# Mixing before projecting in a graph attention layer, with scores as dot products on VectorE and a new deadline for the list scheduler

## The chip, the cores and the metric

The kernel runs on one core of a Trainium2 chip. Times are device microseconds (us) of that core; a smaller number is better. The kernel before took 2403.49 us, the median of 3 runs (2402.94 to 2405.41). The names of lines (L404) are line numbers of the kernel that the profile belongs to; up to L576 the lines that matter have the same number in both.

## The reference, cut to what matters

The input is 64 graphs of 256 nodes with 256 features, and a 0/1 adjacency per graph. Two layers are applied, each to a normalised and rectified input, each with a residual.

```python
h = relu(layernorm(x))
for i in range(3):                              # layer 0: gated graph network
    m = h @ weight[i]
    aggr = A^T m                                # per graph
    h = gru_cell(aggr, h, w_ih, w_hh, b_ih, b_hh)
x = x + h
h = relu(layernorm(x))                          # layer 1: graph attention
h1 = h @ W.T
e = leaky_relu((h1 @ a_left)[:, None] + (h1 @ a_right)[None, :], 0.2)
alpha = softmax(where(adj == 0, -1e9, e))
x = x + alpha @ h1
```

## The kernel before

Two graphs make a pair; there are 32 pairs, and up to three are in work at once. The pieces that the argument touches follow, in the order of the program. Each call of `pe`, `dve`, `act` or `pool` gives an operation to a list, with an estimate of its cost in ns; nothing is issued then.

```python
# layer 0: split of h for the propagation, on GpSimd           (L495, L497)
pool(530,  ... nc.gpsimd.tensor_copy(nodes(hi)[:, sl, :], nodes(h)[:, sl, :]))
pool(1190, ... nc.gpsimd.tensor_sub(nodes(lo)[:, sl, :], nodes(h)[:, sl, :], nodes(hi)[:, sl, :].bitcast(F32)))
# [...] propagation (L512), then the gated layer's products (L404), summed on
# ScalarE (L411) and VectorE (L414)
# layer 0: the update, for each half db of the features        (L542 to L552)
dve(660,  ... scalar_tensor_tensor(u(), u(), b_h[...], r, op0=ALU.add, op1=ALU.mult))      # L542
dve(V512, ... tensor_add(u(), u(), feats(b)[:, 1, :]))                                       # L545
act(630,  ... activation(u(), u(), AF.Tanh, bias=...))                                       # L547
dve(V512, ... tensor_sub(d(), d(), u()))                                                     # L549
dve(V512, ... tensor_mul(d(), d(), z))                                                       # L550
dve(V512, ... tensor_add(d(), d(), u()))                                                     # L552
# layer 0: the new h back to node layout, 4 transposes a graph (L566)
pe(4 * TR, back, r=[(hT, (g, G + g))], w=[(pt, ONE)])
# [...]
# layer 1: norm, relu, to_features (4 transposes), projection with two score columns
norm_relu(xt, h, g)
to_features(h, hT, g)
pe(4 * 218, proj, r=[(hT, (g, G + g))] + WT, w=[(pm, ONE)])      # h W^T | h (W^T a)
# [...] scores, masked softmax
pe(4 * MM, mix, r=[(pT, ONE), (h1, ks)], w=[(pv, ONE)])          # alpha (h W^T)
```

The order on every engine comes from a list scheduler that runs when the kernel is built. Each operation gets a priority: the deadline of its pair, less the estimated time from the operation to the end of its chain. Among the operations that can start first, the one with the smallest priority goes first. Once built, each engine's order is fixed.

```python
def run(self, deadline):
    for o in reversed(self.ops):
        d = deadline(o.pair)
        for s in o.succs:
            d = min(d, s.prio)
        o.prio = d - o.lat
    # [...] while operations are left: the lowest (start, prio, seq) is placed

order = plan.run(lambda p: 30000.0 * max(p, 0))
```

So the numbers in the deadline are no time that is waited for. They only decide how the work of neighbouring pairs is interleaved. The estimates are constants.

## Time and profile before

| before | value |
|---|---|
| time | 2403.49 us |
| span of the profiled run | 2402.3 us |
| TensorE busy (PE) | 2366.8 us, 99% |
| VectorE busy (DVE) | 1671.0 us, 70% |
| ScalarE busy (ACT) | 1412.9 us, 59% |
| GpSimd busy (POOL) | 536.2 us, 22% |
| TensorE's waits from 100 to 2250 us | 3.2 us in 3 waits |
| one pair in the steady middle | 72.80 us |

In the steady middle one pair leaves the kernel at equal distances. I take the timeline of output transfers, the time from the 2nd to the 29th of them, divided by the 27 intervals: (2221.97 - 256.40) / 27 = 72.80 us. It separates what costs something for each pair from what costs something once, at the start or the end. The same 27 intervals are used for every kernel below.

### The profile page before, as it was taken

The numbers are of one execution on the slowest core, as the hardware profiler recorded it, in microseconds if no ns is written. First come the engines' busy times: TensorE is split into PE (matmuls) and PEld (weight loads), VectorE is DVE, ScalarE is ACT, GpSimd is POOL, SyncE is SP. The second block draws the span as 40 slices with busy tenths as digits, with TensorE's granted clock in tenths as the row PEclk, the third lists the DMA queues.
The fourth block names the chain that finished last, engine by engine and source line by source line (L and its number), as shares of the span: only waits on it lengthen the run. The fifth ranks groups of instructions, "written<-read, shape, count | busy, mean of one in ns | idle before, by whom it ended". The sixth has DMA issues, their size and how long they took to land.

```text
span 2402.3 us, 32347 instructions
## 1 busy us (share of the span) xinstructions
PE 2366.8 (99%) x12385; PEld 2097.8 (87%) x12385; DVE 1671.0 (70%) x3225; ACT 1412.9 (59%) x2757; POOL 536.2 (22%) x582
## 2 busy tenths in 40 slices
PE   8999999999999999999999999999999999999996
PEld 6888888888888888888888888888888888888885
DVE  5577776767676767667677767676767676777774
ACT  5465565665565665566655556655666655666653
POOL 3022222122222122222122222222221222221200
PEclk9999999999999999999999999999999999999998
DMA  3000000000000000000000000000000000000000
GB/s 114 1 10 27 27 27 27 17 11 27 27 27 27 7 21 27 27 27 27 1 27 27 27 27 18 10 27 27 27 27 10 18 27 27 27 19 1 10 9 18
DMA packets 53562, 55.02 MB, mean 23 GB/s; under 512 B 1680, under 2 KB 53408, under 8 KB 53408
## 3 DMA queue, kind: packets, MB, share of 16 engines
q1 hardware_dynamic: 53376, 52.96, 6.6%
q8 instruction: 97, 1.59, 0.3%
q14 instruction: 57, 0.47, 0.1%
q10 hardware_dynamic: 32, 0.01, 0.0%
HBM read 36.18 MB, written 16.78 MB: 22 GB/s over the span
## 4 chain that ended last, share of the span: by engine, by line
PE 96%; DVE 2%; ACT 1%; issue 0%; DMA 0%; POOL 0%; ACTq 0%; DVEq 0%; POOLq 0%
PE bank L404 72%; PE bank L512 7%; PE bank L649 5%; PE bank L594 4%; PE bank L566 4%; PE bank L473 2%; PE bank L640 1%; PE bank L605 1%; PE bank L335 0%; DVE full L552 0%; DVE full L549 0%; DVE small L445 0%; DVE full L550 0%; DVE full L542 0%; ACT full L624 0%
## 5 line engine op out<-in xcount | busy, mean ns | idle before, releaser
L404 PE MATMUL bank<-full,fac 128*128 128x256 f32 x4032 | 1015.2, 379 | 0.0
L404 PE MATMUL bank<-full,fac_hh 128*128 128x256 f32 x4032 | 988.8, 379 | 4.5 <-DVE full L552 3.4
L404 PEld LDWEIGHTS bank<-full,fac 128*128 128x128 f32 x4032 | 752.0, 190 | 95.1 <-DVE full L376 0.4
L404 PEld LDWEIGHTS bank<-full,fac_hh 128*128 128x128 f32 x4032 | 746.5, 190 | 96.8 <-DVE full L552 3.9
L414 DVE TENSOR_TENSOR full<-full,bank 128x512 f32<-128x512 f32 x576 | 386.3, 685 | 419.2 <-PE bank L404 400.2
L411 ACT COPY full<-bank 128x512 f32<-128x512 f32 x576 | 332.9, 584 | 331.7 <-PE bank L404 331.7
L372 POOL TENSOR_TENSOR full<-full 128x512 f32<-128x512 f32 x96 | 124.4, 1296 | 1146.4 <-DVE full L552 1085.0
L528 ACT ACTIVATE full<-full,b_rz 128x512 f32<-128x512 f32 x192 | 135.2, 721 | 222.6 <-DVE full L414 222.6
L512 PE MATMUL bank<-round,round 128*128 128x256 f32 x1536 | 249.1, 305 | 1.7 <-DVE round L576 1.7
L453 POOL TENSOR_TENSOR small<-small,nhalf 128x2 f32<-128x2 f32 x128 | 99.0, 787 | 605.0 <-DVE small L451 603.2
L512 PEld LDWEIGHTS bank<-round,round 128*128 128x128 f32 x1536 | 209.7, 190 | 12.0 <-DVE round L576 1.9
L460 ACT ACTIVATE full<-x,small 128x256 f32<-128x256 f32 x256 | 142.4, 594 | 59.1 <-DVE small L455 59.1
L547 ACT ACTIVATE full<-full,vec 128x512 f32<-128x512 f32 x192 | 133.0, 722 | 64.6 <-DVE full L545 64.3
L549 DVE TENSOR_TENSOR full<-full,full 128x512 f32<-128x512 f32 x192 | 132.0, 688 | 12.3 <-ACT full L547 12.3
L542 DVE SCALAR_TENSOR_TENSOR full<-full,vec,full 128x512 f32<-128x512 f32 x192 | 135.5, 747 | 2.7
L550 DVE TENSOR_TENSOR full<-full,full 128x512 f32<-128x512 f32 x192 | 131.2, 696 | 4.4
L531 ACT ACTIVATE full<-bank,b_rz 128x256 f32<-128x256 f32 x192 | 80.6, 471 | 87.1 <-PE bank L404 86.7
L516 ACT COPY full<-bank 128x512 f32<-128x512 f32 x192 | 109.9, 573 | 32.8 <-PE bank L512 32.8
L552 DVE TENSOR_TENSOR full<-full,full 128x512 f32<-128x512 f32 x192 | 124.6, 689 | 0.1
L545 DVE TENSOR_TENSOR full<-full 128x512 f32<-128x512 f32 x192 | 123.6, 684 | 0.0
L372 DVE TENSOR_TENSOR full<-full 128x512 f32<-128x512 f32 x96 | 66.6, 694 | 81.6 <-ACT full L516 81.6
L566 PE MATMUL bank<-ident,full 128*128 128x128 f32 x768 | 113.5, 277 | 7.1 <-DVE full L552 7.0
(76 smaller groups left out, 2362.2 us busy)
## 6 DMA issues: line engine op xcount, KB each, us to landing
x<-in_x_dram SPq DMA_DIRECT2D x32, 512.0 KB, 3.9
adj<-in_adj_dram SPq DMA_DIRECT2D x32, 512.0 KB, 3.9
out_dram<-x SPq DMA_DIRECT2D x32, 512.0 KB, 2.9
full<-in_L_gnn_w_ih_dram SPq DMA_DIRECT2D x2, 384.0 KB, 5.2
full<-in_L_gnn_weight_dram SPq DMA_DIRECT2D x3, 256.0 KB, 7.0
full<-in_L_gnn_w_hh_dram SPq DMA_DIRECT2D x2, 384.0 KB, 6.8
full<-in_L_gnn_W_dram SPq DMA_DIRECT2D x1, 256.0 KB
rows<-in_L_gnn_a_dram ACTq DMA_DIRECT2D x1, 2.0 KB
```

What stands on the lines that cost most here:

```text
L372: eng.tensor_sub(T.t[:, : 2 * N].rearrange("p (c n) -> p c n", c=2), q[:, :, 1, :], b.t[:, : 2 * N].rearrange("p (c n) -> p c n", c=2))
L404: nc.tensor.matmul(bank.t[:, ts(s, N)], fac[t[0]][:, f, t[1], :], quarter(srcs(t), q), start=(first and n == 0), stop=True, skip_group_che ...
L411: act(A512, lambda: nc.scalar.copy(quarters(dest[e])[:, :, g, :], both(X)), r=[(X, ONE)], w=[(dest[e], (g, 2 + g))])
L414: dve(V512, lambda: nc.vector.tensor_add(quarters(dest[e])[:, :, g, :], quarters(dest[e])[:, :, g, :], both(bank)), r=[(bank, ONE)], w=[(d ...
L460: act(495, lambda k=k, nb=nb: nc.scalar.activation(nodes(dst)[:, k, :], nodes(src)[:, k, :], AF.Relu, bias=sm.t[:, 18 + nb : 19 + nb], sca ...
L512: nc.tensor.matmul(pa.t[:, ts(db, N)], nodes(part)[:, k, ts(db, P)], Ar()[:, k, :], start=(n == 0), stop=(n == len(terms) - 1))
L528: act(630, lambda s=s, RZ=RZ: nc.scalar.activation(feats(RZ[0])[:, s, :], feats(RZ[0])[:, s, :], AF.Sigmoid, bias=b_rz[:, 2 * s : 2 * s + 1]),
L542: dve(660, lambda u=u, db=db, en=en, RZ=RZ: nc.vector.scalar_tensor_tensor(u(), u(), b_h[:, en : en + 1], feats(RZ[db])[:, 0, :], op0=ALU. ...
L547: act(630, lambda u=u, en=en: nc.scalar.activation(u(), u(), AF.Tanh, bias=b_i[:, en : en + 1]), r=[("vec", ONE)], w=[(U[db], (0, 1))])
L549: dve(V512, lambda u=u, d=d: nc.vector.tensor_sub(d(), d(), u()), r=[(U[db], (0, 1))], w=[(hT, q)])
L550: dve(V512, lambda d=d, b=RZ[db]: nc.vector.tensor_mul(d(), d(), feats(b)[:, 1, :]), r=[(RZ[db], (2, 3))], w=[(hT, q)])
L566: nc.tensor.transpose(pt.t[:, (nb * DB + db) * P : (nb * DB + db + 1) * P], feats(hT)[:, db, ts(g * NB + nb, P)], ident)
```

## The change

The intent is to save TensorE work. Since alpha (h W^T) = (alpha h) W^T, the softmax can mix h itself, in node layout, and project afterwards. Then h needs no transposed copy in layer 1. The two scores h (W^T a) become dot products on VectorE, with W^T a spread over all partitions once (`va`). Besides, the deadline gets a slope of 32000 in place of 30000, and the last two pairs get nearly one deadline.

```diff
-            to_features(h, hT, g)
             ks = (g * NB, g * NB + 1)
+            sm = sms[g]
             for nb in range(NB):
 [...]
-                pe(4 * 218, proj, r=[(hT, (g, G + g))] + WT, w=[(pm, ONE)])
-                act(320, lambda pm=pm, k=k: nc.scalar.copy(h1v()[:, k, :], pm.t[:, : D + 2]), ...)
+                for n in range(2):
+                    c = 12 + n * NB + nb
+                    dve(395, lambda ...: nc.vector.scalar_tensor_tensor(
+                        nodes(sc)[:, k, :], nodes(h)[:, k, :], 1.0, va[:, n, :], op0=ALU.mult, op1=ALU.mult,
+                        accum_out=sm.t[:, c : c + 1]), ...)
 [...]
-            pe(4 * MM, mix, r=[(pT, ONE), (h1, ks)], w=[(pv, ONE)])
+            pe(4 * MM, mix, r=[(pT, ONE), (h, ks)], w=[(pg, ONE)])
+            act(A512, lambda ag=ag, pg=pg: nc.scalar.copy(ag.t[:, : DB * N], pg.t), r=[(pg, ONE)], w=[(ag, ONE)])
+            pe(4 * MM, project, r=[(ag, ONE)] + WT, w=[(pv, ONE)])
 [...]
-        order = plan.run(lambda p: 30000.0 * max(p, 0))
+        order = plan.run(lambda p: 32000.0 * (max(p, 0) - 0.7 * max(0, p - (NPAIR - 2))))
```

Cut are the setup of `va` in place of two columns of `wT`, the score operations that now read `sm`, and the renamed buffers.

More of the change, by code (lines that the diff above doesn't have):

```diff
@@ L188, in tile_gated_gnn_then_gat @@
     plan = Plan(WINDOW)
-    WIDE = NBLK * (D + 2)
+    WIDE = NBLK * D
     plan.slot_class("full", [const.tile([P, WIDE], F32, name=f"full{i}") for i in range(23)])
@@ L238, in tile_gated_gnn_then_gat @@
     fac = {m: const.tile([P, 7, 3, P], F32, name=f"fac_{m}") for m in ("hh", 0, 1, 2)}
-    wT = const.tile([P, DB, D + 2], F32, name="wT")
+    wT = const.tile([P, DB, D], F32, name="wT")
+    va = const.tile([P, 2, D], F32, name="va")
     X, ADJ = {}, {}
@@ L344, in setup, with go @@
         transposed(lambda c: wT[:, c, :D], lambda c, r0: ("wT", (c,)), W_n)
-        for db in range(DB):
-            pl = Buf("bank")
-            def go(db=db, pl=pl):
+        pl = Buf("bank")
+        def go():
+            for n in range(2):
                 for ob in range(DB):
-                    nc.tensor.matmul(pl.t[:, 0:2], nodes(Wb)[:, ob, ts(db, P)],
-                                     vec[:, : 2 * DB].rearrange("p (s o) -> p s o", o=DB)[:, :, ob],
+                    c = n * DB + ob
+                    nc.tensor.matmul(pl.t[:, ts(n, D)], vec[:, c : c + 1].to_broadcast([P, P]), nodes(Wb)[:, ob, :],
                                      start=(ob == 0), stop=(ob == DB - 1))
-            pe(440, go, r=[(Wb, ONE), ("vec", ONE)], w=[(pl, ONE)])
-            dve(70, lambda db=db, pl=pl: nc.vector.tensor_copy(wT[:, db, D : D + 2], pl.t[:, 0:2]),
-                r=[(pl, ONE)], w=[("wT", (DB + db,))])
-    WT = [("wT", (0, 1, 2, 3))]
+        pe(4 * MM, go, r=[(Wb, ONE), ("vec", ONE)], w=[(pl, ONE)])
+        dve(V512, lambda: nc.vector.tensor_copy(va, pl.t.rearrange("p (n d) -> p n d", n=2)), r=[(pl, ONE)], w=[("va", ONE)])
+    WT = [("wT", (0, 1))]
     B11, B12, B21, B22 = range(4)
@@ L577, in pair @@
                         nodes(lo)[:, sl, :], pv(), nodes(hi)[:, sl, :].bitcast(F32)), r=[(pt, ONE), (hi, ks)], w=[(lo, ks)])
-        h, hT, h1, sc, pm_ = (Buf("full") for _ in range(5))
-        h1v = lambda: h1.t.rearrange("p (k d) -> p k d", k=NBLK)
+        h, sc, pm_ = (Buf("full") for _ in range(3))
         sms = [Buf("small") for _ in range(G)]
@@ L585, in pair @@
             norm_relu(xt, h, g)
-            to_features(h, hT, g)
             ks = (g * NB, g * NB + 1)
+            sm = sms[g]
             for nb in range(NB):
-                k = g * NB + nb
-                pm = Buf("bank")
-                def proj(pm=pm, g=g, nb=nb):
-                    for db in range(DB):
-                        nc.tensor.matmul(pm.t[:, : D + 2], quarters(hT)[:, db, g, ts(nb, P)], wT[:, db, :],
-                                         start=(db == 0), stop=(db == DB - 1))
-                pe(4 * 218, proj, r=[(hT, (g, G + g))] + WT, w=[(pm, ONE)])
-                act(320, lambda pm=pm, k=k: nc.scalar.copy(h1v()[:, k, :], pm.t[:, : D + 2]), r=[(pm, ONE)], w=[(h1, (k,))])
+                for n in range(2):
+                    c = 12 + n * NB + nb
+                    dve(395, lambda k=g * NB + nb, n=n, c=c, sm=sm: nc.vector.scalar_tensor_tensor(
+                        nodes(sc)[:, k, :], nodes(h)[:, k, :], 1.0, va[:, n, :], op0=ALU.mult, op1=ALU.mult,
+                        accum_out=sm.t[:, c : c + 1]),
+                        r=[(h, (g * NB + nb,)), ("va", ONE)], w=[(sm, (c,)), (sc, (g * NB + nb,))])
@@ L601, in pair, with right @@
             pR = Buf("bank")
-            def right(g=g, pR=pR):
+            def right(sm=sm, pR=pR):
                 for nb in range(NB):
-                    nc.tensor.transpose(pR.t[:, ts(nb, P)],
-                                        h1v()[:, g * NB + nb, D + 1 : D + 2].to_broadcast([P, P]), ident)
-            pe(2 * TR, right, r=[(h1, ks)], w=[(pR, ONE)])
-            for k in ks:
-                act(410, lambda k=k, pR=pR: nc.scalar.activation(
-                    nodes(sc)[:, k, :], pR.t[:, :N], AF.Prelu, bias=h1v()[:, k, D : D + 1], alpha=LEAKY_SLOPE),
-                    r=[(pR, ONE), (h1, (k,))], w=[(sc, (k,))])
+                    c = 12 + NB + nb
+                    nc.tensor.transpose(pR.t[:, ts(nb, P)], sm.t[:, c : c + 1].to_broadcast([P, P]), ident)
@@ L613, in pair @@
+            pe(2 * TR, right, r=[(sm, (14, 15))], w=[(pR, ONE)])
+            for nb, k in enumerate(ks):
+                act(410, lambda k=k, nb=nb, pR=pR, sm=sm: nc.scalar.activation(
+                    nodes(sc)[:, k, :], pR.t[:, :N], AF.Prelu, bias=sm.t[:, 12 + nb : 13 + nb], alpha=LEAKY_SLOPE),
+                    r=[(pR, ONE), (sm, (12 + nb,))], w=[(sc, (k,))])
             sl = slice(g * NB, (g + 1) * NB)
-            sm = sms[g]
-            dve(690, lambda sl=sl: nc.vector.copy_predicated(
+            dve(730, lambda sl=sl: nc.vector.copy_predicated(
@@ L616, in pair @@
                 nodes(pm_)[:, sl, :], nodes(A).bitcast(I32)[:, sl, :], nodes(sc)[:, sl, :]),
                 r=[(A, ks), (sc, ks)], w=[(pm_, ks)])
-            dve(620, lambda sl=sl, sm=sm: nc.vector.tensor_reduce(
+            dve(610, lambda sl=sl, sm=sm: nc.vector.tensor_reduce(
                 sm.t[:, 0:NB], nodes(pm_)[:, sl, :], AX.X, ALU.max, negate=True), r=[(pm_, ks)], w=[(sm, ONE)])
@@ L634, in pair @@
                 r=[(sm, (1,))], w=[(sm, (2,))])
-            pt, pT, pv = Buf("bank"), Buf("full"), Buf("bank")
+            pt, pT, pg, ag, pv = Buf("bank"), Buf("full"), Buf("bank"), Buf("full"), Buf("bank")
             def turn(g=g, pt=pt):
@@ L644, in pair, with mix, project @@
             dve(V512, lambda pt=pt, pT=pT: nc.vector.tensor_copy(pT.t[:, :GN], pt.t), r=[(pt, ONE)], w=[(pT, ONE)])
-            def mix(g=g, pT=pT, pv=pv):
+            def mix(g=g, pT=pT, pg=pg):
+                for db in range(DB):
+                    for jb in range(NB):
+                        nc.tensor.matmul(pg.t[:, ts(db, N)], nodes(h)[:, g * NB + jb, ts(db, P)], pT.t[:, ts(jb, N)],
+                                         start=(jb == 0), stop=(jb == NB - 1))
+            pe(4 * MM, mix, r=[(pT, ONE), (h, ks)], w=[(pg, ONE)])
+            act(A512, lambda ag=ag, pg=pg: nc.scalar.copy(ag.t[:, : DB * N], pg.t), r=[(pg, ONE)], w=[(ag, ONE)])
+            def project(ag=ag, pv=pv):
                 for ib in range(NB):
-                    for jb in range(NB):
-                        nc.tensor.matmul(pv.t[:, ts(ib, D)], pT.t[:, (jb * NB + ib) * P : (jb * NB + ib + 1) * P],
-                                         h1v()[:, g * NB + jb, :D], start=(jb == 0), stop=(jb == NB - 1))
-            pe(4 * MM, mix, r=[(pT, ONE), (h1, ks)], w=[(pv, ONE)])
+                    for db in range(DB):
+                        nc.tensor.matmul(pv.t[:, ts(ib, D)], ag.t[:, db * N + ib * P : db * N + (ib + 1) * P],
+                                         wT[:, db, :], start=(db == 0), stop=(db == DB - 1))
+            pe(4 * MM, project, r=[(ag, ONE)] + WT, w=[(pv, ONE)])
             for nb in range(NB):
```

## The prediction

> **What bounds the kernel now.** I read the page first: engine shares, and the chain that ended last.
>
> ```profile
> PE 2366.8 (99%) x12385; PEld 2097.8 (87%) x12385; DVE 1671.0 (70%) x3225; ACT 1412.9 (59%) x2757; POOL 536.2 (22%) x582
> ...
> PE 96%; DVE 2%; ACT 1%; issue 0%; DMA 0%; POOL 0%; ACTq 0%; DVEq 0%; POOLq 0%
> ```
>
> TensorE covers 99% of the 2402.3 us span and 96% of the chain, so only two things can move the time: the TensorE work itself, and the 2402.3 - 2366.8 = 35.5 us in which TensorE has nothing to do. Which line of the kernel is costly on VectorE or ScalarE matters only if TensorE ends up waiting for it. Next I asked where TensorE's idle time lies. The table of windows (start:end, length, then busy time per engine, granted clock, DMA share, GB/s) has it at the two ends:
>
> ```profile
> 0.00:20.00 20.00, 12.35 (x50) 8.28 (x51) 3.68 (x17) 9.63 (x22) 10.27 (x17) 0.91 0.77 249
> ...
> 2200.00:2250.00 50.00, 50.00 (x265) 44.55 (x264) 35.13 (x68) 29.38 (x57) 10.86 (x12) 1.00 0.03 11
> ...
> 2320.00:2340.00 20.00, 18.50 (x93) 15.60 (x92) 16.73 (x35) 12.25 (x26) 1.34 (x2) 1.00 0.00 1
> 2340.00:2360.00 20.00, 19.75 (x107) 17.13 (x106) 8.98 (x18) 10.25 (x21) 2.75 (x3) 1.00 0.08 27
> 2360.00:2380.00 20.00, 8.45 (x36) 6.42 (x34) 13.06 (x28) 6.85 (x13) 1.34 (x2) 0.69 0.00 0
> 2380.00:2402.30 22.30, 13.82 (x49) 10.17 (x47) 6.10 (x12) 7.60 (x20) 0.00 (x0) 0.81 0.07 24
> ```
>
> The start loses 7.65 us in its first 20 us. The middle is saturated: TensorE's waits between 100 and 2250 us add up to 3.2 us in three waits. From 2320 us on 1.50 + 0.25 + 11.55 + 8.48 = 21.8 us are lost. The timeline of the tail says why: the last gated-layer matmul (L404) of the last pair ends near 2364.1 us, and from there one dependent chain runs alone to 2402.3, that is 38.2 us, alternating between engines:
>
> ```profile
> 2371.75 2.36 PE L566 MATMUL bank<-ident,full 128*128 128x128 f32 x8 [6.84 <-DVE full L552]
> ...
> 2378.68 2.38 PE L473 MATMUL bank<-ident,full 128*128 128x128 f32 x8 [4.57 <-ACT full L460]
> ...
> 2390.22 0.33 PE L640 MATMUL bank<-ident,full 128*128 128x128 f32 x1 [3.06 <-ACT full L624]
> ```
>
> **A trap in the group table.** Its busy column cannot price a TensorE instruction, because the records overlap: the groups of one engine sum to more than its busy time. In a saturated stretch the distance between starts is the price:
>
> ```profile
> 1206.18 1.03 PE L404 MATMUL bank<-full,fac 128*128 128x256 f32 x4
> 1207.04 0.60 PE L566 MATMUL bank<-ident,full 128*128 128x128 f32 x4
> 1207.48 1.46 PE L404 MATMUL bank<-full,fac 128*128 128x256 f32 x6
> ```
>
> Four transposes move the next start by 0.44 us (110 ns each); four L404 records by 0.86 us (215 ns each). Averaged in the same way over the timeline from 300 to 2050 us: 109 ns for a transpose (L473 and L640: 108 to 109), 215.6 ns for an f32 record of 256 columns (L649 and L404), 217.9 ns for one of 258 columns (L594). An f32 matmul is two records (256 L649 matmuls in the program, 512 in the trace), so 431 ns; a transpose is one.
>
> [...] The trace has 427 (L376) and 689 (L552)[...]. The new dot products do ask for the accumulator; no run shows them yet.
>
> **The change part by part, TensorE.** Removed: the second to_features, 8 transposes per pair, 256 in all: 256 x 0.109 = 27.9 us. The projection of h (8 f32 matmuls per pair, 258 columns) becomes the projection of the mixed h (8 matmuls, 256 columns): 512 records x 2.3 ns = 1.2 us saved. The mix keeps 8 matmuls per pair. The row broadcast of the right scores keeps its 4 transposes per pair. Setup gets four matmuls of 256 columns in place of four of 2, some 0.8 us more. Net 27.9 + 1.2 - 0.8 = 28.3 us less TensorE work, all in the saturated stretch but for 0.9 us in the last pair's own tail.
>
> **VectorE and ScalarE.** VectorE gets 8 dot products per pair, 256 in all, over 128x256. By L542 and L376 I take 0.44 us each, and some 0.1 us for reading the accumulator, as ScalarE shows for its own (L624: 187 ns recorded, half hidden). 256 x 0.54 = 138 us, and 1671 becomes about 1810 us, 76% of the span. ScalarE loses 64 copies of the transposes (64 x 0.58 = 37 us) and 128 of the projection (45 us by its row), and gains 64 copies between mix and projection (37 us): about 1368 us. Neither becomes the bound; the work lies beside TensorE's except in the tail. "full" buffers become fewer per pair (hT and h1 go, two copies of the mix come), so buffer waits shouldn't grow.
>
> **The tail.** The built order of the changed kernel shows what the deadline does: both last pairs end their gated layers close together, and behind the last L404 lie the last pair's tail and most of the attention of the pair before: 12 transposes, 8 matmuls of its mix and 8 of its projection, which are 32 records. That is 12 x 0.109 + 32 x 0.2156 = 8.2 us of TensorE work that before stood ahead of that point and now falls into the chain's gaps. The 1.75 us lost at 2320 to 2360 us, which were waits for the same pair's attention, should mostly go too; I count 1.5.
>
> The chain itself, from the last L404, against 38.2 us before: VectorE now has the other pair's two copy_predicated (0.73 each) and two reduces (0.69) between L545 and L549, two dot products ahead of that, and a PSUM copy (0.68) behind: about +4.5 us until relu. From relu to the scores, transposes, copies and projections (2378.7 to 2386.8) become dot products that start behind each relu: 8 x 0.44 = 3.5 us, about 3.5 us less. The exps need no table load of their own (31 loads in the program for 32 before): -1.3. After the mix come a copy and the projection: 0.6 + 0.2 for the copy, 1.9 for the half that isn't overlapped: +2.7. Sum +2.4: a tail of about 40.5 us.
>
> **Sum.** The last L404 ends at 2364.1 - 27.4 (the saving outside the last tail) - 8.2 - 1.5 = 2327.0 us. I add 2 us for new waits in the middle, since VectorE's queue is fuller and its order was made for 0.395 us per dot product. With the tail: 2327.0 + 2 + 40.5 = 2369.5 us of span. The device time lies 1.2 us over the span (2403.49 against 2402.3): 2370.7, so 2371 us, 1.4% faster.
>
> **Rivals.** First, *VectorE becomes felt*. [...] For it:[...] the fixed order of the queue, which cannot move a late instruction aside. Against it: in the saturated middle VectorE waits 400 us in all for L404's banks, so it has room. [...] Second, *the tail gains more*: if the two pairs' chains overlap without queueing, the tail stays at 36 us or less and the time is 2364 to 2366. For it: the last 38 us hold 20 us of idle TensorE. Against it: the chain is one pair's dependences, and the other pair's work is queued in front of it on VectorE. Third, *a transpose is worth less than 109 ns*[...]. The distances between starts speak against it.
>
> **Range and chances.** The removed work is well priced (28 us, give or take 2); tail and new waits carry the doubt, some 10 us to each side, more upward. Range 2358 to 2386. Over 2% faster means below 2355.4, another 15 us of idle: 0.06. Over 2% slower would need VectorE to become the bound: 0.01. Within 2%: 0.93.
>
> **What would show it.** In the changed profile: TensorE busy near 2338 us with 256 L473 records; dot products of 0.4 to 0.5 us; TensorE waits in the middle below 6 us; the last L404 near 2329 us and 38 to 43 us behind it. I'm wrong if waits in the middle pass 15 us, if the dot products take 0.7 us, or if the tail leaves 36 to 46 us.

The sum came to 2327.0 + 2 + 40.5 = 2369.5 us of span, 2371 us of device time. The first rival's slower dot product and the third's cheaper transpose gave 2384 us each; neither was shown. (The 0.7 us among the tests at the end is the first rival's.) 427 and 689 are ns for 256 and 512 elements; L542 takes 747 ns for 512 in the trace. The trace of the kernel before shows:

- TensorE's groups add up to 2757 us of busy time, where the engine has 2366.8.
- Half of the accumulator's read by ScalarE (L624) is hidden: its 187 ns begin 94 ns before the activation ahead of it ends.
- A table load takes 1.283 us.
- The two-column matmuls of the setup (L350) start 111 ns apart. Eight records at 215.6 in place of eight at 111 make 0.84 us, the 0.8 of the sum.

The 2 us for new waits and the 0.2 us beside the copy are my estimates, with no line of the trace for them. That VectorE's queue keeps its order when an instruction is late is shown by two runs told below: the 20 instructions from an L414 to an L571 come in the same sequence in alg_only (from 996.22 us) and in late_casts (from 976.62), though two L549 take 0.69 and 0.68 us in the one, 1.76 and 1.75 in the other.

## The result, and the profile after

The changed kernel took 2448.16 us, the median of 6 runs (2446.94 to 2449.18), against 2403.44 for the kernel before in its 6 runs. The ratio is 1.0184, with a 95% interval of 1.0171 to 1.0197. A ratio here is the mean time of one kernel's fast runs over that of the other's of the same rounds, so it is not quite the ratio of the medians. The result is correct. The kernel is 1.8% slower, where 1.4% faster was predicted: 77 us over the prediction and 62 us beyond the range.

First the engine shares and the chain that ended last, of the kernel after:

```profile
PE 2369.6 (97%) x12129; PEld 2061.8 (84%) x12129; DVE 1790.4 (73%) x3736; ACT 1342.6 (55%) x2627; POOL 548.0 (22%) x582
...
PE 76%; DVE 18%; ACT 4%; issue 1%; DMA 0%; POOL 0%; ACTq 0%; DVEq 0%; POOLq 0%
```

TensorE runs the 256 matmul records fewer that it should (12129 for 12385). But 18% of the chain is now on VectorE, where it was 2%. The end of the program does not explain this. The last gated-layer matmuls are in TensorE's timeline:

```profile
2404.03 2.32 PE L404 MATMUL bank<-full,fac 128*128 128x256 f32 x10
```

The last of these ends near 2406.3 us of a span of 2446.6: a tail of 40.3 us, where 40.5 was predicted. The whole miss lies ahead of it: 2406.3 - 2329 = 77 us. Between 100 and 2260 us TensorE has these waits (the line it waits at, what it waits for, us in total, times, longest):

```profile
PE bank L566 <- DVE full L552: 43.9, 55, 1.3
PE bank L473 <- ACT full L460: 5.8, 1, 5.8
```

The first comes twice in each pair, about 1.3 us and then 0.3 us, all along: TensorE waits for the last step of the update before it can turn h back. By the output transfers a pair takes (2267.24 - 253.46) / 27 = 74.58 us, where 72.80 less the predicted saving of 0.90 would be 71.90. So 2.68 us are lost with each pair. The groups of VectorE instructions say which are longer (busy us, mean ns of one, then idle time before them); first before, then after:

```profile
L549 DVE TENSOR_TENSOR full<-full,full 128x512 f32<-128x512 f32 x192 | 132.0, 688 | 12.3 <-ACT full L547 12.3
L550 DVE TENSOR_TENSOR full<-full,full 128x512 f32<-128x512 f32 x192 | 131.2, 696 | 4.4
L545 DVE TENSOR_TENSOR full<-full 128x512 f32<-128x512 f32 x192 | 123.6, 684 | 0.0
```

```profile
L545 DVE TENSOR_TENSOR full<-full 128x512 f32<-128x512 f32 x192 | 166.6, 894 | 2.2
...
L550 DVE TENSOR_TENSOR full<-full,full 128x512 f32<-128x512 f32 x192 | 152.8, 823 | 2.2
...
L549 DVE TENSOR_TENSOR full<-full,full 128x512 f32<-128x512 f32 x192 | 139.6, 742 | 2.2 <-ACT full L547 2.2
```

These three lines are not touched by the change, and each does the same work as before. Yet the means rose by 210, 127 and 54 ns. There are 6 of each per pair, so 6 x 0.391 = 2.35 us per pair. The means mix two kinds: only one of the three updates of a pair is hit. Counted from the records of the trace, 56 of the 192 L545 have an L495 or L497 of GpSimd beside them for over 0.1 us and take 1400 ns in the mean; the others take 686. The new instructions, which I had watched, are as cheap as expected:

```profile
L591 DVE SCALAR_TENSOR_TENSOR full<-full,va 128x256 f32<-128x256 f32 x256 | 93.7, 420 | 19.8 <-ACT full L460 18.7
```

Here is one update in VectorE's timeline (start, duration, instructions in a row), before:

```profile
1004.60 1.42 DVE L542 SCALAR_TENSOR_TENSOR full<-full,vec,full 128x512 f32<-128x512 f32 x2
1005.93 1.29 DVE L545 TENSOR_TENSOR full<-full 128x512 f32<-128x512 f32 x2
1007.40 0.69 DVE L549 TENSOR_TENSOR full<-full,full 128x512 f32<-128x512 f32 x1 [0.19 <-ACT full L547]
1008.13 0.69 DVE L550 TENSOR_TENSOR full<-full,full 128x512 f32<-128x512 f32 x1
...
1010.07 1.29 DVE L552 TENSOR_TENSOR full<-full,full 128x512 f32<-128x512 f32 x2
```

and after:

```profile
1005.85 1.62 DVE L542 SCALAR_TENSOR_TENSOR full<-full,vec,full 128x512 f32<-128x512 f32 x2
1007.38 2.78 DVE L545 TENSOR_TENSOR full<-full 128x512 f32<-128x512 f32 x2
1010.08 1.09 DVE L549 TENSOR_TENSOR full<-full,full 128x512 f32<-128x512 f32 x1
1011.21 1.64 DVE L550 TENSOR_TENSOR full<-full,full 128x512 f32<-128x512 f32 x1
1012.77 0.68 DVE L549 TENSOR_TENSOR full<-full,full 128x512 f32<-128x512 f32 x1
1013.49 0.69 DVE L550 TENSOR_TENSOR full<-full,full 128x512 f32<-128x512 f32 x1
1014.10 1.29 DVE L552 TENSOR_TENSOR full<-full,full 128x512 f32<-128x512 f32 x2
```

From the start of L542 to the end of L552 it is 11.36 - 4.60 = 6.76 us before and 15.39 - 5.85 = 9.54 after. What else ran from 1007 to 1012 us? GpSimd's timeline of the kernel after:

```profile
1007.24 0.69 POOL L495 CAST round<-full 128x512 fp32r<-128x512 f32 x1 [4.25 <-ACT full L460]
1008.01 1.60 POOL L497 TENSOR_TENSOR round<-full,round 128x512 fp32r<-128x512 f32 x1
1009.56 1.07 POOL L495 CAST round<-full 128x512 fp32r<-128x512 f32 x1
1010.71 1.59 POOL L497 TENSOR_TENSOR round<-full,round 128x512 fp32r<-128x512 f32 x1
```

The four stand beside the long instructions of VectorE. As soon as the last one has ended, at 1012.3 us, L549 and L550 are back at 0.68 and 0.69. In the kernel before, the first pair of this group ran 10 us ahead of the update:

```profile
994.51 0.61 POOL L495 CAST round<-full 128x512 fp32r<-128x512 f32 x1 [2.42 <-ACT full L460]
995.20 1.27 POOL L497 TENSOR_TENSOR round<-full,round 128x512 fp32r<-128x512 f32 x1
```

There VectorE was idle, or in L414, which has one source in PSUM. An L414 that started at 995.49, within this L497, took 0.69 us, its usual time.

Nor was this one an exception: in the kernel before, 58 of the 576 L414 have an L495 or L497 beside them for over 0.1 us and take 688 ns in the mean, the others 684. In the kernel after, L549 and L550 with one beside them (27 of each) take 1092 and 1646 ns, the others 684 and 688. By the program L545, L549 and L550 have two inputs in SBUF, L414 has one, and L495 and L497 read SBUF. That two-input instructions of VectorE and instructions of GpSimd that read SBUF hold each other up was the theory, not shown so far, and the experiments had to show whether it carries the time.

### The profile page after: what moved, and what is told of

It reads as the page before. It is cut to its first block, busy times and chain, and to the rows that moved or that the text cites. A ratio compares the mean times of both kernels' runs of the same rounds, so it can differ in the third digit from the quotient of the medians.

```text
span 2446.6 us, 32271 instructions
## 1 busy us (share of the span) xinstructions
PE 2369.6 (97%) x12129; PEld 2061.8 (84%) x12129; DVE 1790.4 (73%) x3736; ACT 1342.6 (55%) x2627; POOL 548.0 (22%) x582
## 4 chain that ended last, share of the span: by engine, by line
PE 76%; DVE 18%; ACT 4%; issue 1%; DMA 0%; POOL 0%; ACTq 0%; DVEq 0%; POOLq 0%
PE bank L404 53%; PE bank L512 7%; PE bank L644 5%; PE bank L653 5%; PE bank L566 3%; DVE full L545 3%; DVE full L550 3%; DVE full L549 2%; DVE full L414 2%; DVE small L445 2%; DVE full L542 1%; ACT full L528 1%; PE bank L473 1%; PE bank L635 1%; DVE full L552 1%
## 5 line engine op out<-in xcount | busy, mean ns | idle before, releaser
L404 PE MATMUL bank<-full,fac_hh 128*128 128x256 f32 x4032 | 1024.2, 381 | 1.5 <-ACT full L411 1.5
L404 PE MATMUL bank<-full,fac 128*128 128x256 f32 x4032 | 1022.8, 380 | 0.1
L404 PEld LDWEIGHTS bank<-full,fac_hh 128*128 128x128 f32 x4032 | 746.8, 190 | 114.2 <-ACT full L411 22.1
L404 PEld LDWEIGHTS bank<-full,fac 128*128 128x128 f32 x4032 | 748.2, 190 | 103.0 <-DVE full L376 8.9
L414 DVE TENSOR_TENSOR full<-full,bank 128x512 f32<-128x512 f32 x576 | 378.5, 683 | 331.1 <-PE bank L404 308.1
L411 ACT COPY full<-bank 128x512 f32<-128x512 f32 x576 | 329.2, 583 | 356.6 <-PE bank L404 353.6
L372 POOL TENSOR_TENSOR full<-full 128x512 f32<-128x512 f32 x96 | 123.3, 1285 | 775.6 <-DVE full L552 594.2
L512 PE MATMUL bank<-round,round 128*128 128x256 f32 x1536 | 247.1, 303 | 1.8 <-DVE round L576 1.7
L512 PEld LDWEIGHTS bank<-round,round 128*128 128x128 f32 x1536 | 207.6, 190 | 18.1 <-DVE round L576 9.4
L528 ACT ACTIVATE full<-full,b_rz 128x512 f32<-128x512 f32 x192 | 129.0, 720 | 133.6 <-DVE full L414 133.4
L576 DVE TENSOR_TENSOR round<-bank,round 128x512 fp32r<-128x512 f32 x128 | 85.8, 689 | 118.1 <-ACT round L574 118.0
L545 DVE TENSOR_TENSOR full<-full 128x512 f32<-128x512 f32 x192 | 166.6, 894 | 2.2
L534 ACT ACTIVATE full<-full,b_rz 128x256 f32<-128x256 f32 x192 | 91.1, 506 | 138.2 <-DVE full L414 137.8
L566 PE MATMUL bank<-ident,full 128*128 128x128 f32 x768 | 114.2, 278 | 45.3 <-DVE full L552 45.2
L550 DVE TENSOR_TENSOR full<-full,full 128x512 f32<-128x512 f32 x192 | 152.8, 823 | 2.2
L566 PEld LDWEIGHTS bank<-ident,full 128*128 128x128 f32 x768 | 91.1, 141 | 72.9 <-DVE full L552 62.7
L542 DVE SCALAR_TENSOR_TENSOR full<-full,vec,full 128x512 f32<-128x512 f32 x192 | 140.8, 748 | 10.0
L460 ACT ACTIVATE full<-x,small 128x256 f32<-128x256 f32 x256 | 136.0, 592 | 14.8 <-DVE small L455 14.6
L549 DVE TENSOR_TENSOR full<-full,full 128x512 f32<-128x512 f32 x192 | 139.6, 742 | 2.2 <-ACT full L547 2.2
```

What stands on the lines that cost most here:

```text
L404: nc.tensor.matmul(bank.t[:, ts(s, N)], fac[t[0]][:, f, t[1], :], quarter(srcs(t), q), start=(first and n == 0), stop=True, skip_group_che ...
L411: act(A512, lambda: nc.scalar.copy(quarters(dest[e])[:, :, g, :], both(X)), r=[(X, ONE)], w=[(dest[e], (g, 2 + g))])
L414: dve(V512, lambda: nc.vector.tensor_add(quarters(dest[e])[:, :, g, :], quarters(dest[e])[:, :, g, :], both(bank)), r=[(bank, ONE)], w=[(d ...
L460: act(495, lambda k=k, nb=nb: nc.scalar.activation(nodes(dst)[:, k, :], nodes(src)[:, k, :], AF.Relu, bias=sm.t[:, 18 + nb : 19 + nb], sca ...
L512: nc.tensor.matmul(pa.t[:, ts(db, N)], nodes(part)[:, k, ts(db, P)], Ar()[:, k, :], start=(n == 0), stop=(n == len(terms) - 1))
L528: act(630, lambda s=s, RZ=RZ: nc.scalar.activation(feats(RZ[0])[:, s, :], feats(RZ[0])[:, s, :], AF.Sigmoid, bias=b_rz[:, 2 * s : 2 * s + 1]),
```

## The experiments

**The theory (C, collision).** The slope of 32000 moved GpSimd's casts and subtractions beside the update, both read SBUF, and the update is where TensorE then waits. **Rival V:** VectorE's queue is longer by the dot products, and the update comes late because of them. **Rival A:** the new algebra itself (the copy between mix and projection, fewer transposes for other work to hide behind) costs more than it saves. **Rival D:** the deadline is worse by itself, through the order on all engines, whatever GpSimd does. **Rival G:** it is not the reading, but simply that GpSimd is busy at that time.

All times in this table are medians, the ratio is to the kernel before on the same chip. The medians of before in the three groups of runs were 2404.28, 2404.61 and 2403.54 us. "Wrong" means a wrong result on purpose.

| kernel | us | ratio | us per pair | result |
|---|---|---|---|---|
| before | 2403.44 | 1 | 72.80 | correct |
| after | 2448.16 | 1.0184 | 74.58 | correct |
| alg_only | 2391.21 | 0.9945 | 71.90 | correct |
| deadline_only | 2415.8 | 1.0049 | 73.58 | correct |
| pool_blank | 2391.05 | 0.9943 | 72.53 | wrong |
| short_dots | 2446.76 | 1.0177 | 74.58 | wrong |
| slope30_tail | 2378.76 | 0.9890 | 71.90 | correct |
| slope32_flat | 2459.95 | 1.0229 | 74.60 | correct |
| pool_busy | 2390.55 | 0.9938 | 72.54 | wrong |
| late_casts | 2502.99 | 1.0408 | 75.11 | correct |
| after_late | 2422.9 | 1.0078 | 72.54 | correct |
| slope28_tail | 2391.01 | 0.9948 | 72.40 | correct |
| slope34_tail | 2424.97 | 1.0088 | 73.64 | correct |

### alg_only: the new algebra with the old deadline

```diff
-order = plan.run(lambda p: 32000.0 * (max(p, 0) - 0.7 * max(0, p - (NPAIR - 2))))
+order = plan.run(lambda p: 30000.0 * max(p, 0))
```

> The changed algebra with the old deadline (30000 per pair, no bend for the last two pairs). In the changed kernel a pair takes 74.58 us in the middle against 72.80 before and the 71.9 I had predicted, and TensorE waits for L552 once in each pair. If the new deadline made the order in which this happens, the middle falls to about 71.9 us per pair and the time to about 2376 us (27 us under before). If the algebra does it in any order, the time stays at 2445 to 2455 us.

It took 2391.21 us, ratio 0.9945 (0.9928 to 0.9961). A pair takes 71.90 us, 0.90 less than before. That is what the prediction's TensorE sum makes per pair, (27.9 + 1.2) / 32 = 0.91. The time missed the expected 2376 all the same: the middle gains 27 x 0.90 = 24 us, but the second output leaves 8.3 us later than in the kernel before (264.69 against 256.40), and from the 29th output to the end it is 3.8 us longer (184.1 against 180.3). L545, L549 and L550 are at 684, 689 and 693 ns. There is a collision in this order too: the dot products (L591) have a mean of 574 ns, and in the pair near 1015 us two of eight took 1.31 and 0.93 us beside GpSimd's L372 and L378, the others 0.41 or 0.42. TensorE waits for none of them from 300 to 2000 us. Rival A falls for the middle: the algebra gains there what it should, and the order is what takes it away.

### deadline_only: the kernel before with the new deadline

```diff
-order = plan.run(lambda p: 30000.0 * max(p, 0))
+order = plan.run(lambda p: 32000.0 * (max(p, 0) - 0.7 * max(0, p - (NPAIR - 2))))
```

> The kernel before with nothing but the new deadline. If the new slope of the deadline is to blame, this kernel gets the wait too, up to 2.7 us per pair, 2450 to 2480 us. If the algebra is to blame, it stays near 2400 us, a few us under or over before, by the tail alone.

It took 2415.8 us, ratio 1.0049 (1.0034 to 1.0064), 73.58 us per pair: 0.78 more than before. That is neither of the two times expected. L545, L549 and L550 stay at 691, 684 and 686 ns, so there is no collision here. Weight loads wait for other things (19.5 us for L376 in 47 waits, from 300 to 2000 us). Algebra alone is -0.90 per pair and the deadline alone +0.78; together they would be -0.12, but they measure +1.78. So 1.90 us per pair belong to neither part by itself, only to both together. Rival D holds for a smaller part.

### pool_blank: the same order, but GpSimd no longer reads

```diff
-pool(530, ... nc.gpsimd.tensor_copy(nodes(hi)[:, sl, :], nodes(h)[:, sl, :]), ...
+pool(530, ... nc.gpsimd.memset(nodes(hi)[:, sl, :].bitcast(F32), 0.0), ...
-pool(1190, ... nc.gpsimd.tensor_sub(nodes(lo)[:, sl, :], nodes(h)[:, sl, :], nodes(hi)[:, sl, :].bitcast(F32)), ...
+pool(1190, ... nc.gpsimd.memset(nodes(lo)[:, sl, :].bitcast(F32), 0.0), ...
```

The estimates given to the scheduler are kept, so the order on all engines is that of the kernel after. The moment is not: the cast waits for ScalarE's relu (L460, 4.25 us in the lines above), a memset of zeros doesn't, and so the memsets run earlier. The result is wrong (relative error 0.32).

> The changed kernel in exactly its own order on every engine, wrong on purpose: GpSimd's cast (L495) and subtraction (L497) of the first layer write zeros by memset, so that they read nothing from SBUF and are shorter. Theory 1, GpSimd and VectorE hinder each other: L545 falls from a mean of 894 ns to under 720, L550 from 823 to under 720, TensorE's wait for L552 nearly goes, the pair takes 72 to 72.5 us, the time is 2370 to 2385 us. Theory 2, VectorE is late because it has eight dot products more per pair: 2435 us or more.

It took 2391.05 us, ratio 0.9943 (0.9928 to 0.9958), and 72.53 us per pair: 2.05 of the 2.68 us are gone. (The time is 6 us above the range expected.) The group of L545, and TensorE's waits from 100 to 2260 us, of which those at L566 have nearly vanished (43.9 us in the kernel after):

```profile
L545 DVE TENSOR_TENSOR full<-full 128x512 f32<-128x512 f32 x192 | 126.6, 687 | 2.2
```

```profile
PE bank L473 <- ACT full L460: 6.0, 2, 5.8
PE bank L566 <- DVE full L552: 0.2, 1, 0.2
```

So the loss goes when GpSimd's casts and subtractions are not beside the update. But a memset is shorter than a subtraction (518 ns in the mean, where L497 took 1562 in the kernel after), and in the trace only one of the 192 L545, and no L549 or L550, has a memset beside it. This run therefore does not tell the reading from being busy: rival G is open until after_late.

### short_dots: dot products over 8 columns in place of 256

```diff
-nodes(sc)[:, k, :], nodes(h)[:, k, :], 1.0, va[:, n, :], op0=ALU.mult, op1=ALU.mult,
+nodes(sc)[:, k, :8], nodes(h)[:, k, :8], 1.0, va[:, n, :8], op0=ALU.mult, op1=ALU.mult,
```

The order is again that of the kernel after; the result is wrong (relative error 0.053).

> The changed kernel in exactly its own order, wrong on purpose: each dot product covers 8 columns instead of 256, which takes some 0.25 us off each, 2 us of VectorE per pair. Theory 1 (GpSimd and VectorE hinder each other in L545 to L550): the stretched instructions stay stretched, L545 above 850 ns, the time stays above 2435 us. Theory 2 (VectorE is late by the added dot products): TensorE's wait for L552 shrinks by up to 2 us per pair, 2380 to 2395 us.

It took 2446.76 us, ratio 1.0177 (1.0161 to 1.0192). The dot products fell from 420 to 165 ns, VectorE's busy time from 1790.4 to 1731.7 us, that is 1.8 us per pair; L545 stays at 894 ns, and the pair still takes 74.58. Rival V falls, and with it the prediction's first rival: the time of the dot products is not felt.

### slope30_tail: the new algebra, the old slope, the tail's bend kept

```diff
-order = plan.run(lambda p: 32000.0 * (max(p, 0) - 0.7 * max(0, p - (NPAIR - 2))))
+order = plan.run(lambda p: 30000.0 * (max(p, 0) - 0.7 * max(0, p - (NPAIR - 2))))
```

> The changed kernel with the old slope of the deadline (30000 per pair) and the new bend for the last two pairs: the order of the middle should be that of alg_only, which takes 71.90 us per pair. With alg_only's middle and a tail of some 40 us behind the last L404 with the other pair's attention in its gaps, as the changed kernel has it, I expect 2372 to 2380 us, faster than both kernels. If the bend is worth nothing, 2391 us as alg_only.

It took 2378.76 us, ratio 0.989 (0.9876 to 0.9905), and is correct. It beats both kernels. A pair takes 71.90 us, as in alg_only, and the bend gains 2391.21 - 2378.76 = 12.5 us at the end. The shares of its profile:

```profile
PE 2340.2 (98%) x12129; PEld 2076.6 (87%) x12129; DVE 1729.6 (73%) x3736; ACT 1378.6 (58%) x2627; POOL 520.6 (22%) x582
```

TensorE's busy time is where the prediction put it (near 2338), with the same 12129 records that read 2369.6 in the kernel after. So busy time that includes stalls of this kind is not a count of work.

### slope32_flat: the new algebra, the new slope, no bend

```diff
-order = plan.run(lambda p: 32000.0 * (max(p, 0) - 0.7 * max(0, p - (NPAIR - 2))))
+order = plan.run(lambda p: 32000.0 * max(p, 0))
```

> The changed kernel with the new slope (32000) and without the bend. If the slope alone makes the bad order in the middle, a pair takes 74.58 us as in the changed kernel, and with the longer tail of alg_only the time is 2455 to 2465 us. If the bend is what makes it, the middle falls to about 71.9 us per pair, some 2391 us.

It took 2459.95 us, ratio 1.0229, and 74.60 us per pair. The slope alone makes the bad middle, with or without the bend. The bend is worth 2459.95 - 2448.16 = 11.8 us here, much as with the other slope.

### pool_busy: GpSimd as long busy as before, still not reading

```diff
-pool(530, ... nc.gpsimd.memset(nodes(hi)[:, sl, :].bitcast(F32), 0.0), ...
+pool(530, ... [nc.gpsimd.memset(nodes(hi)[:, sl, :].bitcast(F32), 0.0) for _ in range(2)], ...
-pool(1190, ... nc.gpsimd.memset(nodes(lo)[:, sl, :].bitcast(F32), 0.0), ...
+pool(1190, ... [nc.gpsimd.memset(nodes(lo)[:, sl, :].bitcast(F32), 0.0) for _ in range(3)], ...
```

This diff is against pool_blank, and the result is wrong in the same way.

> As pool_blank, in the same order, wrong on purpose, but GpSimd is kept busy as long as with the casts: two memsets of 128x512 in place of each L495, three in place of each L497 (a memset took 518 ns). If what hinders is GpSimd's reading and writing of two tensors beside VectorE's two (theory 1), the time stays at 2391 us and L545 under 720 ns. If GpSimd's time itself delays something, or its writes hinder as much, 2420 us or more.

It took 2390.55 us, ratio 0.9938 (0.9922 to 0.9955), and 72.54 us per pair, the same as pool_blank. L545, L549 and L550 are at 687, 687 and 689 ns. GpSimd spent as much time on the memsets of L497 (100.8 us) as on the real instructions in the kernel after (100.0 us).

The same time is not in the same place, though: these memsets don't wait for L460 either, and run earlier. In the trace 57 of the 192 L545 have a memset beside them, and these take 684 ns in the mean (688 without one); no L549 or L550 has one. Rival G is answered here for L545 alone.

### late_casts: the collision put into the good order

```diff
-pool(530, ... nc.gpsimd.tensor_copy(nodes(hi)[:, sl, :], nodes(h)[:, sl, :]), ...
+pool(530, ... ([nc.gpsimd.memset(nodes(hi)[:, sl, :].bitcast(F32), 0.0) for _ in range(24 * (1 - g))],
+               nc.gpsimd.tensor_copy(nodes(hi)[:, sl, :], nodes(h)[:, sl, :])), ...
```

This is alg_only with 24 memsets ahead of the first cast of each pair. They write what the cast overwrites, so the result stays right. The order on the other engines is alg_only's, and only the casts run later, into the update.

> The converse, with a right result: alg_only in exactly its own order, where GpSimd's casts run at a time when VectorE reads PSUM or nothing; 24 memsets ahead of the first cast of each pair push them some 13 us back, to where VectorE is at L542 to L552. Theory 1: L545, L549 and L550 are stretched (means of 740 to 900 ns, against 684 to 693 in alg_only), TensorE's wait for L552 appears, up to 2 us per pair, 2405 to 2450 us. Otherwise 2391 us, as alg_only.

It took 2502.99 us, ratio 1.0408 (1.0392 to 1.0423), 75.11 us per pair against alg_only's 71.90. That is more than the 2405 to 2450 us expected. L549 rose to a mean of 1005 ns, L545 to 755, L550 to 728, and TensorE's waits at L566 for L552 are 59.7 us in 54. In the timelines of VectorE and of GpSimd one sees a whole instruction put behind another:

```profile
986.16 1.76 DVE L549 TENSOR_TENSOR full<-full,full 128x512 f32<-128x512 f32 x1
...
988.86 1.75 DVE L549 TENSOR_TENSOR full<-full,full 128x512 f32<-128x512 f32 x1
```

```profile
985.77 1.60 POOL L497 TENSOR_TENSOR round<-full,round 128x512 fp32r<-128x512 f32 x1
...
988.47 1.60 POOL L497 TENSOR_TENSOR round<-full,round 128x512 fp32r<-128x512 f32 x1
```

L549 takes 1.76 us in place of 0.69; GpSimd's L497, undisturbed 1.27 us, takes 1.60. Both of these L549 end only after the L497 beside them (987.92 after 987.37, and 990.61 after 990.07). So the collision can be made, too, in an order that had next to none in the update. Not all of the 112 us over alg_only is the collision: 27 x 3.21 = 87 us is in the steady middle, and of the rest 23 us lie ahead of the second output (287.58 us against 264.69), where TensorE waits for the delayed casts themselves (L512 for L495, 13.0 us in one wait). Nor are the 87 us all of one kind. In this run alone TensorE's granted clock falls in the middle (the mean of the run is 0.980, alg_only's 0.991): 11 times in the 27 intervals it is 0.5 for 3.4 us, as at 390.6 us, behind a wait of 1.94 us, and there L404 records start 0.43 us apart in place of 0.216. That loses 11 x 1.7 = 19 us, or 0.70 per pair. The other 2.51 are what the three instructions grew by: 6 x (0.316 + 0.071 + 0.035) = 2.53. Why the clock fell was not tested.

### after_late: the collision taken out of the bad order

The same edit as in late_casts, applied to the kernel after, with 19 memsets: the casts now start when L552 has ended.

```diff
+pool(530, ... ([nc.gpsimd.memset(nodes(hi)[:, sl, :].bitcast(F32), 0.0) for _ in range(19 * (1 - g))],
+               nc.gpsimd.tensor_copy(nodes(hi)[:, sl, :], nodes(h)[:, sl, :])), ...
```

> The changed kernel in its own order and with a right result, but with more work for GpSimd: 19 memsets of 128x512 ahead of the first cast of each pair, some 10 us, so that the casts start when L552 is about done instead of beside L545 to L550. Theory 1 (GpSimd's two-tensor work holds VectorE's two-tensor work up): the wait for L552 goes and the time falls to 2388 to 2400 us, as in pool_blank and pool_busy, though GpSimd does more. If it is the amount of GpSimd's work, 2448 us or more. The risk is that the casts come too late for L512 or hold the next L372 up.

The time missed the expectation: 2422.9 us, ratio 1.0078 (1.0061 to 1.0095), not 2388 to 2400. But the pair takes 72.54 us, exactly as in pool_busy, with the right result, and L545, L549 and L550 are near 693 ns. What GpSimd does beside the update here is writing only, from before L542 to behind L552 (GpSimd first, then VectorE):

```profile
1002.64 11.01 POOL L495 MEMSET round<- 128x512 f32 x19
...
1007.10 1.29 DVE L545 TENSOR_TENSOR full<-full 128x512 f32<-128x512 f32 x2
1009.00 0.69 DVE L549 TENSOR_TENSOR full<-full,full 128x512 f32<-128x512 f32 x1 [0.62 <-ACT full L547]
```

In the trace 57 of the L545, 54 of the L549 and 54 of the L550 have a memset beside them, with means of 684, 688 and 692 ns. So GpSimd busy at that time costs nothing if it only writes: rival G falls here, and what is left is that L495 and L497 read. The 32 us over pool_busy lie at the ends. The second output leaves at 273.62 us, against 253.60 in pool_busy (20 us). From the 29th output to the end it is 188.6 us against 177.4 (11 us). There the delayed casts hold up the propagation: TensorE waits at L512 for L495, 16.0 us in two waits, and the granted clock is lower (0.96 in the first 300 us, 0.99 in pool_busy; 0.991 and 0.996 over the whole runs). So the theory holds for the middle, and my expectation left out that a delay that is free in the middle isn't at the ends.

### slope28_tail and slope34_tail: is 30000 a good number, or 32000 a bad one?

```diff
-order = plan.run(lambda p: 32000.0 * (max(p, 0) - 0.7 * max(0, p - (NPAIR - 2))))
+order = plan.run(lambda p: 28000.0 * (max(p, 0) - 0.7 * max(0, p - (NPAIR - 2))))    # slope28_tail
+order = plan.run(lambda p: 34000.0 * (max(p, 0) - 0.7 * max(0, p - (NPAIR - 2))))    # slope34_tail
```

> The changed kernel with a deadline of 28000 per pair, bend kept. A third order of the middle. If the length of the middle hangs on where the order happens to put GpSimd's casts, it can be 71.9 us per pair (2375 to 2380 us) or up to 74.6 (2448 us), and L545 to L550 tell which: means under 700 ns with the first, over 740 ns with the second. A slow middle with all of them under 700 ns would mean that there is another cause of the same size.

> As slope28_tail with 34000 per pair: a fourth order, the same question. A slow middle with L545, L549 and L550 under 700 ns would mean another cause of the same size.

With 28000 it took 2391.01 us (72.40 per pair, update at 684 to 687 ns), which is neither outcome expected: a quiet update, but 0.50 over slope30_tail. The collision has moved: VectorE's L376 has a mean of 694 ns (425 in the kernel after), and 27 of its 96 records, beside an L497, take 1378. No wait of TensorE from 300 to 2000 us is put down to it, so what makes the 0.50 is not shown. With 34000 it took 2424.97 us (73.64 per pair). Per pair the four slopes 28000, 30000, 32000 and 34000 give 72.40, 71.90, 74.58 and 73.64: the time is no smooth function of the slope. At 34000 another collision appears. L549 and L550 rise to 775 and 767 ns, in the trace beside GpSimd's right factors (L372 to L378), of which L376 and L378 are long, too. On GpSimd L376 has a mean of 911 ns. In the kernel after it takes 736 ns, in the kernel before 839, where nothing waits for it. Here TensorE's weight loads wait for L378, which follows it on GpSimd: 26.6 us in 23 waits from 300 to 2000 us. TensorE also waits for ScalarE (L404 for L411, 22.3 us in 30 waits from 100 to 2250 us). What of the 1.74 us over slope30_tail is due to which I have not separated.

## Why the prediction was wrong, point by point

**TensorE's work: right.** alg_only and slope30_tail save 0.90 us per pair, which is the sum of the prediction. Its third rival (a transpose worth less than 109 ns) would have shown here, and fell.

**VectorE and ScalarE: VectorE's size right by luck, ScalarE's right, the conclusion wrong.** The dot products take 420 ns where I took 440, and 81 ns to read the accumulator where I took 100. VectorE's busy time is 1790 us (predicted 1810), ScalarE's 1343 (1368). VectorE's figure includes some 75 us of stalls (2.35 x 32), which pool_blank does not have (1713.5 us). So the added work was priced nearly 100 us too high, by chance hidden by the stalls. About half of it is overlap: consecutive dot products with their reads start 0.345 us apart, where I took 0.54, and 256 x 0.195 = 50 us. Another 30 us is L455, which fell from 48.8 us before to 18.4 after and which the prediction left out. "Neither becomes the bound; the work lies beside TensorE's except in the tail" was true of the totals, and says nothing of a chain of six instructions that ends where TensorE waits.

**The tail: right in its sum, in part by luck.** 40.3 us against 40.5. The second rival (36 us or less) fell. In the traces the stretch from the last L404 to the first relu (L460) grew by 2.3 us (predicted 4.5), that from there to the first exp fell by 4.5 (predicted 3.5 + 1.3 = 4.8), and the rest grew by 5.1 (predicted 2.7): two errors of over 2 us cancel. Three readings were off without moving the sum much. The last L404 before ends at 2364.9 us by its record (2362.59 + 2.32; the line is not shown), not 2364.1, which shifts 0.8 us between the tail and the work ahead of it. The 3.5 us between relu and scores would be 8.1 - 3.5 = 4.6 by the times it cites. And the 1.2 us between span and device time joined two different runs: the profiled run itself took 2405.27 us for its span of 2402.3.

**The step that failed: "I add 2 us for new waits in the middle".** The term measures 2.68 us per pair, 72 us over the 27 intervals alone, and 77 us in all up to the last L404. The prediction's own test, that it is wrong if the waits in the middle pass 15 us, was met: they are 49.7 us. The path that it had wrong is the update's: the step took VectorE's instructions at their old durations in the new order. The reason given for the 2 us, a fuller queue on VectorE, is not what happened, as short_dots shows. In its place:

- 2.05 us per pair are the collision. Moving the reading away from the update, with GpSimd writing in its place and the right result, gives 72.54 (after_late); pool_blank and pool_busy, where GpSimd reads nothing there but also runs earlier, give 72.53 and 72.54. Putting the reading into the good order costs 3.21 (late_casts), of which 0.70 go with the lower clock and 2.51 with the stretched instructions. This is shown from both sides.
- 0.63 us per pair (72.53 - 71.90) remain in the order of the slope of 32000 without this collision. In the kernel after, weight loads wait from 300 to 2000 us as follows:

```profile
PEld bank L566 <- DVE full L552: 50.8, 46, 1.7
PEld bank L404 <- ACT full L411: 16.6, 46, 0.4
PEld bank L404 <- DVE full L376: 6.1, 22, 0.3
PEld bank L512 <- DVE round L576: 5.8, 23, 0.3
```

The last three are in pool_blank too, at much the same size (16.5, 6.4 and 6.1), while alg_only, slope30_tail and the kernel before have no such wait at all. They add up to 28.5 us over some 23 pairs, more than 0.63 each, so part of them is hidden. That they are the 0.63 is a reading of the trace; no run took them away one by one.

Why the prediction missed it: GpSimd was given no line in it, because its 22% looked harmless. I looked at the built order only for the tail, where the bend was meant to act, and took the slope, 30000 to 32000, for a detail. The bend did what the change wanted (12 us), but the slope did harm in all the pairs.

**What remains of the distance with the good order.** slope30_tail is 7.8 us over the predicted 2371. Its last L404 ends near 2335.3 us, 6.3 later than predicted, and its tail is 42.2 us, 1.7 longer; these make 8.0. The first part has a wait in the trace that the kernel before does not have at that size: L473 waits for L460 once, 7.5 us, in the first 260 us. Its cause I did not test. Nor did I separate the cast (L495) from the subtraction (L497) in the collision.

## What to carry to other kernels

Here the price of an instruction held only for the neighbours it was measured with: L545 takes 686 ns, and 1400 with an L495 or L497 beside it. In the kernel after its records go from 670 to 1757 ns, with a median of 691 and a mean of 894, and the mean is what the chain pays. When a change moves the order, look for what now runs beside the instructions that end in a wait of the bounding engine, also on engines that are mostly idle. If the mean of an instruction that was not edited changes, put the timelines of all engines at that moment side by side. Change the algebra and a scheduler's constant in separate runs, and try neighbouring values of the constant before you judge either.
